# Gated cross-attention and mixture-of-experts block: nine groups in place of ten, scores of two early groups as eight feature planes summed by TensorE, late value sums in pairwise additions, and a planner that counts VectorE's dependent instructions apart

## The chip, the cores and the metric

The kernel runs on one core of a Trainium2 chip. The metric is device time in microseconds (us) of one execution; a kernel's time is the median of several executions. The engines are named TensorE (PE in the profile; PEld is its weight load), VectorE (DVE), ScalarE (ACT), GpSimd (POOL) and SyncE (SP), which here issues most transfers.

## The reference

The input is 8192 tokens of 128 features, and a context of the same shape. Each token is normalised and attends, **within itself**, over 16 heads of 8 features: query head i sees key heads 0 to i of its own token's context. The result, times tanh of a gate, is added to the token. Then comes a feed-forward part on the normalised sum: one shared expert for all tokens, and 8 experts of which each token takes its two best.

```
qh = layernorm(x).reshape(B, S, 16, 8);  kh = vh = ctx.reshape(B, S, 16, 8)
scores = einsum("bsqd,bskd->bsqk", qh, kh) / sqrt(8), causal over the 16 heads
x = x + tanh(g_xattn) * (softmax(scores) @ vh)
xf = layernorm(x);  logits = xf @ router_w.T + bias;  two best, softmax of the two
x = x + tanh(g_ffn) * (shared(xf) + sum over the two best e of w_e * expert_e(xf))
expert(z) = (silu(z @ w1) * (z @ w3)) @ w2        # 128 -> 256 -> 128
```

All is float32.

## The kernel before

**Groups.** The tokens are cut into groups; a group holds J tokens in each of the 128 partitions (J is 4 or 8, so a group is 512 or 1024 tokens). `STAGES` and `DENSE` (lines 32 and 33) list the J of each: stage 0 is 4, 4, 8, 8, 8, stage 1 is 8, 8, 8, 4, and one dense group of 4 comes last, ten groups in all, numbered 0 to 9.

**Attention** (`attention`, line 587). The causal 16 x 16 head pairs are taken as squares of side s = 8, 4, 2, 1 (half of them lies in the later heads, `late`), and the diagonal, called level 0: 136 pairs per token, in 1088 products. For each square VectorE multiplies query by key into a tile `pr` of up to 2048 columns (from a packed copy `qc` of the queries, made by ScalarE), and reduces over the 8 features into `sc` by a second VectorE instruction. For a group in `EARLY` (line 1298: group 2) the products are written feature by feature instead (`spread`), and TensorE sums them: eight matmuls with the identity into one PSUM tile, which ScalarE copies to `sc`. After the softmax's maxima and exponentials VectorE multiplies the weights by the values (`valued`, line 709, again into `pr`), and TensorE adds these up into the PSUM tile `o`, one identity matmul per key. For the pairs of group and level in `ON_DVE` (line 1307) VectorE reduces over the keys first, by a strided reduction into a tile `hb`, and TensorE adds only the totals.

**Rest of a group** (`rest`, line 866): output, second norm, transposes, router, then the shared expert in pieces of 512 tokens. The reciprocal root of a norm runs on GpSimd (`pow`), or, for the entries of `NEWTON` (line 1304), as eleven small VectorE instructions. `dispatch` gives each token copy its slot; 2J indirect transfers issued by GpSimd put the rows into the region `xs` of their expert.

**Blocks.** `plan` (line 1021) finds out, by a chain of small VectorE instructions, which blocks of 128 rows are complete. `block_pair` (line 1105) handles two blocks: SyncE fetches rows `xb` and the expert's weights `wb` (384 KB a block), TensorE transposes and multiplies, ScalarE applies silu and scales the result `yb`, and GpSimd puts the rows to `ys` by two indirect transfers. Blocks become available group by group: 8, 16, 16, 32 after groups 1 to 4, and 8, 16, 16, 24 after groups 5 to 8 (lines 418 to 426), 136 in all. When a stage's last group has been planned, `finish` (line 1222) adds `ys` into each group's tokens, two accumulating transfers per group, and stores them. The dense group runs all eight experts on all of its tokens, with `xT` at hand, and needs no dispatch.

**Order.** Every operation is recorded with an engine, a modelled duration and a priority, and `Recorder.order` (line 152) writes the order of every engine's instructions at build time: on each engine it starts the ready operation of the lowest priority value. A priority is a time in units of one group of 8 (`when`, line 1248), plus offsets by kind (`NORM`, `STATS`, `PLAN`, `BLOCKS`, `PUT`, `REST`, `SHARED`, `DLAG` and `DSTEP`) and by hand (`SHIFT`, line 1311). The engines run these orders as written; each waits in order. A buffer pool (`CT`, `PR`, `PM`, `YB` and others, line 1300) bounds how far ahead they may run.

Of the kernel before, what the change touches and what calls it, by code (L numbers as in the profile page):

```python
# [20 lines left out]
P = 128  # L21
# [10 lines left out]
STAGES = [[4, 4, 8, 8, 8], [8, 8, 8, 4]]  # L32
# [5 lines left out]
NORMED = [[0], [1], [2], [3, 4], [5, 6], [7, 8, 9]]  # L38
# [72 lines left out]
class Op:  # L111
    def __init__(self, eng, emit, us, lat, prio, table, size):
        self.eng, self.emit, self.us, self.lat = eng, emit, us, lat
        self.prio, self.table, self.size = prio, table, size
        self.deps, self.behind, self.next, self.new = set(), set(), [], []
        self.ins, self.start, self.end = [], None, None
        self.put = False


class Recorder:  # L120
# [6 lines left out]
    def add(self, eng, emit, us, r=(), w=(), after=(), behind=(), lat=0.06, table=None, size=0):  # L127
        self.prio += 1e-5
        op = Op(eng, emit, us, lat, self.prio, table, size)
# [22 lines left out]
    def order(self):  # L152
# [30 lines left out]
        while len(done) < len(self.ops):  # L183
# [43 lines left out]
            for n in op.next:  # L227
                same = n.eng == op.eng and not op.size
                ready[n] = max(ready[n], t + us if same or op in n.behind else op.end)
                todo[n] -= 1  # L230
                if not todo[n]:
                    wait[n.eng].append(n)
# [11 lines left out]
def kernel(  # L244
# [66 lines left out]
    def fixed(eng, handle, base, per):  # L311


        class Calls:
            def __getattr__(self, method):
                def call(out, *a, n=0, us=None, table=None, behind=(), **k):
                    w = [out] + ([k["accum_out"]] if "accum_out" in k else [])
                    r = list(a) + [v for name, v in k.items() if name != "accum_out"]
                    return record(
# [4 lines left out]
                        us if us is not None else base + per * n,  # L324
                        r, w, table=table, behind=behind,
# [4 lines left out]

    V = fixed(DVE, nc.vector, 0.13, 1.045e-3)
    A = fixed(ACT, nc.scalar, 0.14, 0.88e-3)
    G = fixed(POOL, nc.gpsimd, 0.2, 2.4e-3)

# [180 lines left out]
    tabled = record(DVE, tables, 2.5, [], [])  # L515
# [4 lines left out]
    def stats(parts, which):  # L520
# [10 lines left out]
        def sums(fn, dst, **k):  # L531
            i = 0
            for g, src, scratch in parts:
                for j in range(JS[g]):
# [3 lines left out]
                        to, src[:, j, :], fn, accum_out=dst[:, i : i + 1].part(g), us=0.4,  # L538
                        **bias, **k,
# [27 lines left out]
    def normed(dst, src, g, rs, mb):  # L567
        for j in range(JS[g]):
            A.activation(
                dst[:, j, :], src[:, j, :], AF.Identity,  # L570
                bias=mb[:, j : j + 1], scale=rs[:, j : j + 1], us=0.4,
# [4 lines left out]
    def first_norm(g):  # L576
        q_[g] = buf("q", [P, JM, D])[:, : JS[g]]
        normed(q_[g], xs_[g], g, *norms.pop(g))
# [8 lines left out]
    def attention(g):  # L587
        J = JS[g]
        first = len(R.ops)
        q, ct = q_.pop(g), ct_.pop(g)  # L590
        sc = buf("sc", [P, JM * NS])

        qc = {}
        for s in (8, 4, 2):
            qc[s] = buf(f"qc{s}", [P, JM * NH // 2, HD], bufs=1)[:, : J * NH // 2]
            A.copy(
                qc[s].rearrange("p (t s) d -> p t s d", s=s), halves(q, s)[0], n=J * D // 2
            )
# [11 lines left out]
        def spread(pr, pattern, **k):  # L610


            if g in EARLY:
                pr = pr.rearrange("p (d n) -> p n d", d=HD)
                return pr.rearrange("p (a k) d -> p a k d", **k) if k else pr
            return pr.rearrange(pattern, d=HD, **k)

        def summed(dst, pr, n):

            if g not in EARLY:  # L620
                pr = pr.rearrange("p (n d) -> p n d", d=HD)
                V.tensor_reduce(dst, pr, AX.X, ALU.add, n=n * HD)
                return

            acc = psum("m", [P, n], PM)
            matmuls(
                [
                    (acc, ident, pr[:, d * n : (d + 1) * n], d == 0, d == HD - 1)
                    for d in range(HD)
                ],  # L630
                1.75e-3 * n * HD,
            )
            A.copy(dst, acc, n=n)

        for s in SQ:
            T = J * NH // (2 * s)
            n = T * s * s
            parts = max(1, n * HD // PRW)
            hi, lo = halves(q, s)[0], halves(ct, s)[1]
            for h in range(parts):  # L640
                t0, tn = h * T // parts, T // parts
                a0, an = h * n // parts, n // parts
                pr = products()[:, : an * HD]
                if s > 1:
                    V.tensor_tensor(
                        spread(pr, "p (a k d) -> p a k d", k=s),
                        qc[s][:, t0 * s : (t0 + tn) * s]
                        .unsqueeze(2).to_broadcast([P, tn * s, s, HD]),
                        lo[:, t0 : t0 + tn]
                        .rearrange("p t k d -> p t (k d)")  # L650
                        .unsqueeze(2)
                        .to_broadcast([P, tn, s, s * HD]),
                        ALU.mult, n=an * HD,
                    )
                else:
                    V.tensor_tensor(
                        spread(pr, "p (t d) -> p t d"), hi[:, :, 0], lo[:, :, 0],
                        ALU.mult, n=an * HD,
                    )
                summed(level(sc, s)[:, a0 : a0 + an], pr, an)  # L660
        pr = products()[:, : J * D]
        (G if g in ON_POOL else V).tensor_tensor(
# [707 lines left out]
```

## Time and profile before

| | us |
|---|---|
| median of 9 runs (684.32 to 695.59) | 690.8 |
| the profiled execution | 687.88 |
| its span | 686.2 |
| TensorE busy | 542.2 |
| VectorE busy | 484.6 |
| GpSimd busy | 361.2 |
| ScalarE busy | 342.7 |

The mean clock granted to TensorE was 0.916 of full speed. The span begins with the first instruction and ends with the last, so 1.7 us of the execution lie around it.

The page gives busy time by engine and by fortieths of the span. Other views used below: the table of stretches (busy time of each engine in given windows, with the granted clock, the share of the transfer engines and their rate), the groups of instructions by form (mean duration of one), the order of time, and the chain that ended last. Groups are written `out<-in`. Nearly all instructions carry line 321 or 345, the helpers that record them, so tiles identify them.

### The profile page before, as it was taken

The page shows a single profiled execution, that of the slowest core. Times are in us where ns is not written, and L with a number is a line of the kernel's source. Part 1 is how long each engine was busy: PE and PEld are TensorE (multiplying, and loading weights), DVE is VectorE, ACT ScalarE, POOL GpSimd, SP SyncE. Part 2 cuts the span into 40 slices and gives each one's busy share as a digit, 9 for nine tenths or more (in the row PEclk, how much of TensorE's full clock was granted, in tenths as well). Part 3 has the DMA queues.
Part 4 walks back from the last instruction along what each step waited for, and adds up shares of the span by engine and source line. Part 5 has one row for each costly group of instructions (what it writes and reads, how often), then busy time and mean ns, then how long its engine had stood idle before and what let it go on. Part 6 is the DMA issues. An engine that isn't in the chain of part 4 may idle for free.

```text
span 686.2 us, 10993 instructions
## 1 busy us (share of the span) xinstructions
PE 542.2 (79%) x3247; PEld 450.2 (66%) x3247; DVE 484.6 (71%) x964; ACT 342.7 (50%) x1085; POOL 361.2 (53%) x342
## 2 busy tenths in 40 slices
PE   0075977968958977998797289996776879999997
PEld 0053865856846767796587278885564778988764
DVE  1698938999987995799597077999964863423343
ACT  6277467186158275856662028826433515544321
POOL 2020744526824874478758734577676374555440
PEclk9996987979989998999899589999787999999999
DMA  9710200521366227621868147489375388888095
GB/s 166 257 31 0 106 19 25 188 78 36 127 217 208 62 92 226 204 100 40 260 191 263 56 124 240 154 168 269 118 217 174 126 270 261 276 271 277 26 174 164
DMA packets 62716, 107.34 MB, mean 156 GB/s; under 512 B 10137, under 2 KB 34216, under 8 KB 62656
## 3 DMA queue, kind: packets, MB, share of 16 engines
q1 hardware_dynamic: 51424, 82.88, 38.8%
q0 software_dynamic: 10784, 23.74, 12.8%
q8 instruction: 26, 0.43, 0.3%
q14 instruction: 34, 0.28, 0.1%
q10 hardware_dynamic: 448, 0.01, 0.0%
HBM read 85.48 MB, written 25.31 MB: 161 GB/s over the span
## 4 chain that ended last, share of the span: by engine, by line
PE 41%; DVE 18%; POOL 13%; DMA 8%; issue 7%; another core or an unknown queue 5%; ACT 5%; SPq 3%; POOLq 0%; DVEq 0%; ACTq 0%
PE m L345 14%; PE gp L345 10%; PE up L345 10%; POOL xs L842 8%; DVE pr L321 5%; PE o L345 5%; DMA x<-ys 3%; DVE sc L321 2%; PE m L343 2%; DVE hb L321 2%; ACT xm L321 2%; POOL rsaw L321 1%; SPq L507 1%; POOL ys L1205 1%
## 5 line engine op out<-in xcount | busy, mean ns | idle before, releaser
L842 POOL DMA_INDIRECT xs<-xm,slot x120 | 158.9, 1324 | 65.7 <-issue 35.4
L345 PE MATMUL o<-pr,ident 128*128 128x256 f32 (+1 forms) x452 | 118.0, 414 | 33.9 <-DVE pr L321 33.5
L1205 POOL DMA_INDIRECT ys<-yb,xb x80 | 86.9, 1086 | 92.3 <-ACT yb L321 73.6
L345 PEld LDWEIGHTS o<-pr,ident 128*128 128x128 f32 x452 | 87.4, 200 | 50.8 <-DVE pr L321 32.7
L321 ACT ACTIVATE sg<-gp 128x512 f32<-128x512 f32 x116 | 68.7, 596 | 91.5 <-PE gp L345 43.4
L321 DVE TENSOR_TENSOR hb<-sg,up 128x512 f32<-128x512 f32 x68 | 46.3, 684 | 78.0 <-remote 19.9
L345 PE MATMUL m<-wb,hb 128*128 128x128 f32 x544 | 79.1, 293 | 25.5 <-DVE hb L321 7.6
L345 PEld LDWEIGHTS m<-wb,hb 128*128 128x128 f32 x544 | 71.8, 203 | 39.8 <-ACT xbT L321 9.2
L1205 POOL DMA_INDIRECT ys<-yb,seen x56 | 62.4, 1114 | 62.1 <-ACT yb L321 52.0
L345 PE MATMUL gp<-xbT,wb 128*128 128x128 f32 x544 | 78.5, 291 | 16.6 <-issue 13.1
L345 PEld LDWEIGHTS gp<-xbT,wb 128*128 128x128 f32 x544 | 72.0, 206 | 20.5 <-issue 14.3
L321 DVE TENSOR_TENSOR pr<-sc,ct 128x2048 f32<-128x2048 f32 (+3 forms) x56 | 79.1, 1441 | 4.8 <-ACT sc L321 2.9
L345 PE MATMUL up<-xbT,wb 128*128 128x128 f32 x544 | 74.9, 282 | 3.9 <-DVE hs L321 3.9
L321 ACT ACTIVATE yb<-m,xb 128x128 f32<-128x128 f32 x136 | 42.4, 363 | 60.6 <-PE m L345 38.6
L345 PEld LDWEIGHTS up<-xbT,wb 128*128 128x128 f32 x544 | 69.4, 199 | 4.6 <-DVE hs L321 4.1
L321 DVE TENSOR_REDUCE sc<-pr 128x256 f32<-128x2048 f32 (+3 forms) x50 | 71.0, 1420 | 1.0
L321 DVE TENSOR_TENSOR pr<-qc,ct 128x2048 f32<-128x2048 f32 (+2 forms) x36 | 70.1, 1953 | 0.0
L321 DVE TENSOR_TENSOR hs<-sg,up 128x512 f32<-128x512 f32 x48 | 32.3, 683 | 21.8 <-PE up L345 11.8
L321 ACT COPY qc<-q 128x512 f32<-128x512 f32 (+1 forms) x30 | 15.4, 533 | 62.5 <-DVE pr L321 62.4
L343 PE MATMUL m<-ident,xb 128*128 128x128 f32 x136 | 27.9, 284 | 21.4 <-DMA xb<-xs 13.6
L321 ACT COPY xbT<-m 128x256 f32<-128x256 f32 x68 | 24.4, 371 | 38.3 <-PE m L343 22.3
L345 PEld LDWEIGHTS m<-w2s,hs 128*128 128x128 f32 x256 | 36.2, 222 | 7.6 <-issue 5.2
(157 smaller groups left out, 897.6 us busy)
## 6 DMA issues: line engine op xcount, KB each, us to landing
wb<-wall SPq DMA_DIRECT2D x136, 384.0 KB
xb<-xs SPq DMA_DIRECT2D x136, 65.0 KB
x<-ys POOLq DMA_DIRECT2D x12, 512.0 KB
x<-in_x_dram SPq DMA_DIRECT2D x6, 512.0 KB
ct<-in_ctx_dram SPq DMA_DIRECT2D x6, 512.0 KB
out_dram<-x SPq DMA_DIRECT2D x6, 512.0 KB
pr<-wall SPq DMA_DIRECT2D x8, 384.0 KB
wall<-in_L_ffn_w_dram SPq DMA_DIRECT2D x2, 1024.0 KB
```

What stands on the lines that cost most here:

```text
L321: lambda: getattr(handle, method)(real(out), *[real(v) for v in a], **{q: real(v) for q, v in k.items()}),
L343: got.append(nc.tensor.transpose(o, a, b))
L345: got.append(nc.tensor.matmul(o, a, b, start=j[3], stop=j[4]))
L507: nc.sync.dma_start(out=wall[:, :, 2 * H + c * D : 2 * H + (c + 1) * D], in_=w2[:, c * P : (c + 1) * P, :],)
L842: ins = nc.gpsimd.indirect_dma_start(out=xs[s][:, :], out_offset=bass.IndirectOffsetOnAxis(ap=real(slot[:, i : i + 1]), axis=0), in_=real( ...
L1205: ins = nc.gpsimd.indirect_dma_start(out=ys[s][:, :], out_offset=bass.IndirectOffsetOnAxis(ap=real(ids[i]), axis=0), in_=real(yb[:, i, :]) ...
```

## The change

- `STAGES` becomes 4, 8, 8, 8 and 8, 8, 8, 8, with the dense group of 4 last: nine groups, 0 to 8. Blocks become available as 16, 16, 32 after groups 1 to 3 and 8, 16, 16, 32 after groups 4 to 7, 136 in all.
- `EARLY` is groups 1 and 2. For these, `first_norm` writes the queries with the feature outermost, ScalarE copies the keys in the same order, and `planes_scores` multiplies plane by plane; TensorE sums the eight planes of a level in one PSUM tile.
- `ON_DVE` goes. `PRE` lists, by group and level, how many rounds of pairwise additions VectorE does on `pr`, in place, each halving what TensorE adds.
- The three buffers `qc` become one; `ON_POOL`, which was empty, goes; pieces of the shared expert adapt to J.
- The planner: a VectorE or ScalarE operation's modelled time is now 0.085 or 0.09 us shorter towards an independent successor, and 0.05 us longer than its full time towards one on the same engine that depends on it (`own`). Some modelled durations change.
- `NEWTON` for the second norms grows from groups 0, 2, 6, 8 to groups 1, 2, 4, 5, 6, 7, 8. `YB` goes from 6 to 5. All offsets and `SHIFT` are replaced.

```diff
-STAGES = [[4, 4, 8, 8, 8], [8, 8, 8, 4]]
+STAGES = [[4, 8, 8, 8], [8, 8, 8, 8]]
-NORMED = [[0], [1], [2], [3, 4], [5, 6], [7, 8, 9]]
+NORMED = [[0], [1], [2, 3], [4, 5], [6, 7, 8]]
...
                 same = n.eng == op.eng and not op.size
-                ready[n] = max(ready[n], t + us if same or op in n.behind else op.end)
+                if op in n.behind:
+                    then = t + us
+                elif same:
+                    then = t + us + op.own
+                else:
+                    then = op.end
+                ready[n] = max(ready[n], then)
...
+                    early = 0.0 if "accum_out" in k else own
...
-                        us if us is not None else base + per * n,
-                        r, w, table=table, behind=behind,
+                        (us if us is not None else base + per * n) - early,
+                        r, w, table=table, behind=behind, own=early + 0.05, lat=early + 0.06,
...
-    V = fixed(DVE, nc.vector, 0.13, 1.045e-3)
-    A = fixed(ACT, nc.scalar, 0.14, 0.88e-3)
+    V = fixed(DVE, nc.vector, 0.15, 1.045e-3, 0.085)
+    A = fixed(ACT, nc.scalar, 0.14, 0.88e-3, 0.09)
...
     def first_norm(g):
...
+        q = q_[g].rearrange("p j x -> p (j x)").rearrange("p (d j s) -> p d j s", d=HD, j=J)
+        rs, mb = norms.pop(g)
+        for j in range(J):
+            A.activation(
+                q[:, :, j, :], xs_[g][:, j, :].rearrange("p (s d) -> p d s", d=HD), AF.Identity,
+                bias=mb[:, j : j + 1], scale=rs[:, j : j + 1], us=0.57,
+            )
...
+        def planes_scores():
+            qd = q.rearrange("p j x -> p (j x)")
+            cd = buf("qc", [P, 3, JM * NH // 2, HD], bufs=1).rearrange("p i t d -> p (i t d)")[:, : J * D]
+            A.copy(
+                cd.rearrange("p (d t) -> p d t", d=HD),
+                ct.rearrange("p j (t d) -> p d (j t)", d=HD), n=J * D,
+            )
+            for s in [*SQ, 0]:
+                n = J * (PAIRS[s] if s else NH)
+                acc = psum("m", [P, n], PM)
+                parts = max(1, n * HD // PRW)
+                w = HD // parts
+                for h in range(parts):
+                    pr = products()[:, : n * w]
+                    a, b = (t[:, h * w * J * NH : (h + 1) * w * J * NH] for t in (qd, cd))
+                    if s:
+                        a, b = (
+                            t.rearrange("p (x w s) -> p x w s", w=2, s=s)[:, :, i]
+                            for t, i in ((a, 1), (b, 0))
+                        )
+                        X = w * J * NH // (2 * s)
+                        if s > 1:
+                            a = a.unsqueeze(3).to_broadcast([P, X, s, s])
+                            b = b.unsqueeze(2).to_broadcast([P, X, s, s])
+                            pr4 = pr.rearrange("p (x q k) -> p x q k", q=s, k=s)
+                        else:
+                            pr4 = pr.rearrange("p (x s) -> p x s", s=1)
+                        V.tensor_tensor(pr4, a, b, ALU.mult, n=n * w)
+                    else:
+                        V.tensor_tensor(pr, a, b, ALU.mult, n=n * w)
+                    matmuls(
+                        [
+                            (
+                                acc, ident, pr[:, d * n : (d + 1) * n],
+                                h == 0 and d == 0, h == parts - 1 and d == w - 1,
+                            )
+                            for d in range(w)
+                        ],
+                        1.7e-3 * n * w + 0.01 * w,
+                    )
+                A.copy(level(sc, s)[:, :n], acc, n=n)
+
+        (planes_scores if g in EARLY else rows_scores)()
...
-                if (g, s) in ON_DVE:
-                    total = buf("hb", [P, PRW // 4], bufs=HB)[:, : an // s * HD]
-                    V.tensor_reduce(
-                        total.rearrange("p (a d) -> p a d", d=HD),
-                        pv.rearrange("p a k d -> p a d k"), AX.X, ALU.add, n=an * HD,
+                for _ in range(PRE.get((g, s), 0)):
+                    terms //= 2
+                    V.tensor_tensor(
+                        pv[:, :, :terms], pv[:, :, :terms], pv[:, :, terms : 2 * terms], ALU.add,
+                        n=an * HD * terms // s,
                     )
...
-EARLY = [2]
+EARLY = [1, 2]
-CT, PR, PM, XB, XR, YB, SG, XT, HB = 2, 5, 2, 4, 6, 6, 2, 2, 2
-PUT, REST = 1.36, 0.69
+CT, PR, PM, XB, XR, YB, SG, XT, HB = 2, 5, 2, 4, 6, 5, 2, 2, 2
+PUT, REST = 0.58, 0.61
-NEWTON = [("b", 0), ("b", 2), ("b", 6), ("b", 8)]
+NEWTON = [("b", 1), ("b", 2), ("b", 4), ("b", 5), ("b", 6), ("b", 7), ("b", 8)]
-ON_DVE = [(7, 8), (8, 2), (8, 8), (9, 4)]
+PRE = {
+    (4, 2): 1, (4, 8): 1, (5, 2): 1, (5, 8): 2, (6, 2): 1,
+    (6, 4): 2, (6, 8): 2, (7, 2): 1, (8, 4): 2, (8, 8): 3,
+}
-NORM, SHARED, BLOCKS = 0.8, 0.3, 0.25
-DSTEP, DLAG, STATS, PLAN = 0.06, 0.78, 1.4, 0.38
+NORM, SHARED, BLOCKS = 1.19, 0.16, 0.33
+DSTEP, DLAG, STATS, PLAN = 0.12, 0.3, 1.42, -0.2
...
```

The `SHIFT` table goes from 22 entries to 23 others; for the blocks of the last planned group it has no entry before (group 8) and -0.27 after (group 7).

## The prediction

> **What bounds the kernel now.** I read the busy times and the fortieths on the page first, then the table of stretches, then the order of time where a stretch looked odd, then the groups by form for durations.
>
> ```profile
> PE 542.2 (79%) x3247; PEld 450.2 (66%) x3247; DVE 484.6 (71%) x964; ACT 342.7 (50%) x1085; POOL 361.2 (53%) x342
> PE   0075977968958977998797289996776879999997
> DVE  1698938999987995799597077999964863423343
> PEclk9996987979989998999899589999787999999999
> ```
>
> No engine is full, and the two rows show why: VectorE is near 9 up to the middle, TensorE from three quarters on. The table of stretches, cut at 525 us, gives the sizes (columns: window, its length, busy us and instructions of each engine, granted clock, transfer share, GB/s):
>
> ```profile
> 0.00:525.00 525.00, 392.58 (x2248) 327.59 (x2249) 410.52 (x776) 278.52 (x927) 290.48 (x271) 0.90 0.47 140
> 525.00:686.20 161.20, 149.64 (x1000) 122.56 (x999) 74.11 (x189) 64.15 (x158) 70.69 (x72) 0.97 0.70 209
> 0.00:126.00 126.00, 71.24 (x303) 56.46 (x304) 86.89 (x188) 74.03 (x306) 43.41 (x59) 0.89 0.30 83
> ```
>
> So there are two regimes. From 525 us on TensorE is idle for only 11.6 us: the end is what TensorE still has to do. Before that it is idle for 132.4 us, and VectorE, busy 78% of the time, sets the pace with its chains. The third row is the start: the first expert block is fetched at 126.4 us, and until then TensorE lacks 55 us of work. A microsecond is gained by getting VectorE through its groups sooner, so that blocks come sooner, or by taking TensorE work out of the end.
>
> One piece belongs to neither. In the order of time VectorE waits twice near 380 us, and the chain that ended last calls both waits unknown:
>
> ```profile
> 373.10 9.16 another core or an unknown queue
> 383.10 13.24 another core or an unknown queue
> ```
>
> Both waits are on TensorE's results, which the profile takes for done at 373.7 us. A shorter one lies at 516.95 us (6.78 us), and one at 422 us (3.8 us). I can't name their cause; the change doesn't address them.
>
> **The change part by part.** Durations are of the profiled execution.
>
> ```profile
> L321 DVE TENSOR_TENSOR pr<-qc,ct 128x2048 f32<-128x2048 f32 x22 | 54.5, 2485 | 0.0
> L321 DVE TENSOR_REDUCE sc<-pr 128x256 f32<-128x2048 f32 x19 | 43.4, 2282 | 0.3
> L321 DVE TENSOR_REDUCE hb<-pr 128x256 f32<-128x2048 f32 x3 | 11.5, 3848 | 0.0
> L321 DVE TENSOR_TENSOR x<-x,xT 128x1024 f32<-128x1024 f32 x6 | 7.3, 1225 | 0.2
> L321 DVE SCALAR_TENSOR_TENSOR rsb<-tb,rsb 128x8 f32<-128x8 f32 x6 | 1.0, 167 | 0.2
> ```
>
> *Scores of groups 1 and 2.* A group of 8 reduces three times 2048 columns (2.28), twice 1024 (1.22) and once 512 (0.68): 9.97 us, which group 1 now gives to TensorE. Group 2 had given it away already, but paid for its layout: its wide products took 3.7 us (order of time, 71.43 to 83.0), against 2.29 for the others, so three times 1.4, plus 0.7 each for two of 1024 columns: 5.7 us. Planes are written in order, so I price them as the ordinary products and take 5.7 off: VectorE -15.7. Bound on the other side: the new inputs are repeated along an axis, which no row shows; if every plane product ran at the rate of the strided reduction (3.85 for 2048), 2 x 4.25 x 1.56 = 13.3 come back, leaving -2.4. I take -15.7, as the old `qc` products also repeat an input and take 2.29. TensorE gets eight planes of 1088 columns: in the end stretch 512 columns step at 0.43 us in two passes each, so 14.6 us; group 2 needed 20.2 us for the same at a lower clock. This lies where TensorE lacks work (the 55 us), so I cost it at nothing; if that cover is gone it is 15 to 20.
>
> *ScalarE* now reads the 16 columns of queries, and writes the key copies, with a stride; no row has that on ScalarE. Below: the 0.49 us of a normal column. Above: the strided VectorE reduction's factor, 1.69, on 16 x 0.49 + 2 x 1.05: 7 us. The three `qc` copies that go (0.62 each) pay for half. ScalarE is busy 53% before 525 us; I take 0, and keep +7. [...]
>
> *Value sums.* One value matmul of 256 columns steps at 0.43 us in its two passes (567.13 to 570.59 for sixteen halves). `ON_DVE` spares TensorE 14+1+7+3 = 25 of them and costs VectorE 14.2 us (11.5+2.0+0.7, the strided rows). `PRE` spares 56 and costs 21 additions; at the row of `x<-x,xT` (1.22 for 1024, 0.69 for 512 columns; a product of 256 takes 0.42) that is 18.1 us. Net: VectorE +3.9, TensorE -13.4, of which 7 matmuls, -3.0, lie in the last groups and so in the full stretch.
>
> *One group fewer.* Groups of 4 took 34 us from output to output (48.9 to 82.8, 466.8 to 500.6), groups of 8 51 to 57; two of 4 cost 68 where one of 8 costs 52. Of the 16 us about 11 are VectorE's fixed part: some 70 instructions (33 attention, 23 routing, 20 planning, less what grows) at 0.16 us, the part that doesn't shrink when 64 columns become 32 (0.22 to 0.19). The other 5 are waits.
>
> *Norms.* Three more chains of eleven at 0.167: VectorE +5.4. The waits of VectorE for GpSimd's second norms (7.7 us in four) mostly go: -2 after what else is late.
>
> *Chains counted apart.* Small dependent instructions start 0.03 us after the one before has ended; the independent `seen` at 382.95 starts 0.09 us before the `hb` of 382.35 ends. So each dependent pair that the planner fills spares 0.12 us; about 40 a group in nine groups make 43 us at most, 0 at least. I take a fifth of the pairs, since the planner must have something ready: -8.6, and at VectorE's part in the pace about -5.
>
> [...]
>
> *Later first blocks, fewer buffers.* Group 1 has 8 columns, so its rows go out later: 18 us more attention (52 against 34), less the 10 of its reductions, plus eight puts at 1.27 us, some 18, bounds 0 and 24. TensorE has the 14.6 us of planes and the larger group's value sums and shared expert (some 12) meanwhile. I take +10, nearer the lower end for that cover. `YB` of 5 lets ten blocks of results, not twelve, wait behind a burst of GpSimd's puts (16 x 1.27 = 20 us); I count that inside the same bound.
>
> **The sum.** VectorE: -15.7 + 3.9 - 11 + 5.4 = -17.4, counted at its 78% share before 525 us: -13.6. Merging's waits -5, chains -5, TensorE's end -3, norm waits -2, late blocks +10: -18.6. From 687.9 for the profiled execution that is 669.3; the median of the runs lies 2.9 higher, so I predict **672 us**.
>
> **The rivals.**
>
> *The end grows (slower).* After the last dispatch 32 blocks are left instead of 24. A pair takes 2.9 us of TensorE in the end stretch (gp, up and m 0.89 each, transposes 0.22), so 8 blocks are 11.6 us. And the stage can only be added up after its last result: before, that took from the last put at 649.70 to the output at about 677, 28 us, hidden under dense experts until 682.9. Dense experts now rank from 8.30 on, the last blocks at 8.50 (before 8.78 and 8.63), so two of eight experts run ahead of them and six, 6 x 5.22 = 31 us, are left as cover. It decides once the last put leaves less than 28 us of dense work behind it: then up to 25 us show, with the 11.6 a time of 700 to 725; I put it at 708. For it: cover shrinks to 3 us. Against it: dense weights come from `wall` at the same rate as before.
>
> *It changes nothing.* TensorE's work is 542 us before and about 543 after (+14.6, -13.4). If the planes end up on the critical path, as they partly did in group 2 (the chain has 8.7 us of its score matmuls at 97 us, at a granted clock of 0.78 in 100 to 125), VectorE's gain turns into a wait for TensorE, and the time stays at 690.
>
> *Much faster.* The unnamed waits of 30 us don't recur and the order fills the chains: 640 to 648.
>
> **How the numbers follow.** The measurement tells about 1% from no change, 684 to 698. Forecast (648 to 684): 0.55; much faster: 0.06; nothing: 0.14; end grows or another loss of its size: 0.25. For 8 in 10 the range takes the forecast, the unchanged case and the lower half of the slow one, up to 708, and stops at 646 below: with all of VectorE's 17.4 (-4), a third of the pairs (-5), no late blocks (-10) and a quarter of the unnamed waits gone (-7). Faster 0.61, same 0.14, slower 0.25.
>
> **What would show it.** Right: `pr` plane products of 2048 columns near 2.3 us; no `hb<-pr` rows, `pr<-pr` additions near 1.2; VectorE near 465 us busy; first block near 145 us; outputs of groups of 8 about 48 us apart; TensorE's full stretch begins near 505 us. Wrong: the last ys put less than 28 us before the end; a stretch before 150 us with TensorE under half busy for longer than now; unknown waits of over 30 us.

## The result, and the profile after

The kernel after takes **706.3 us** (median, 703.22 to 713.59) where the kernel before took 692.0 beside it: the ratio is **1.0241**, with a 95% interval of 1.0217 to 1.0266. The change makes the kernel slower by 2.4%; 672 us was forecast. Ratios, here and below, are of the executions in the faster of the two states that executions show, and need not equal the quotient of two medians. The profiled execution of after has a span of 705.6 us, 19.4 more than before.

Busy time and fortieths of the page of after:

```profile
PE 530.4 (75%) x3233; PEld 432.9 (61%) x3233; DVE 444.3 (63%) x940; ACT 347.1 (49%) x1079; POOL 343.1 (49%) x328
...
PE   0099996856998796398828999951698098999993
...
DVE  1693968999589797099826999960654034232342
```

The table of stretches of after, cut where that of before was cut (window, length, busy us and instructions of PE, PEld, DVE, ACT, POOL, granted clock, transfer share, GB/s):

```profile
0.00:126.00 126.00, 81.88 (x385) 62.05 (x386) 83.02 (x153) 83.21 (x314) 30.64 (x50) 0.97 0.31 87
0.00:525.00 525.00, 384.56 (x2247) 313.35 (x2247) 383.58 (x764) 286.95 (x927) 267.98 (x250) 0.91 0.45 138
525.00:705.60 180.60, 145.88 (x986) 119.51 (x986) 60.76 (x176) 60.16 (x152) 75.13 (x78) 0.92 0.64 192
```

VectorE is busy for 40.3 us less than before, TensorE for 11.8 less and GpSimd for 18.1 less; only ScalarE has 4.4 more. There is less work, and the kernel takes longer. The fortieths (17.6 us each) say where: VectorE's row has 0, 2, 0 and 0 in the slices from 282, 353, 476 and 547 us, and TensorE's row falls to 3, 2, 1 and 0 there. Before has one such place, near 377 us. In order of time, the chain that ended last names them ("another core" can't be meant, since the kernel runs on one: it is a releaser that the profile doesn't show):

```profile
276.35 8.54 another core or an unknown queue
...
286.84 10.68 another core or an unknown queue
...
477.20 20.57 another core or an unknown queue
...
547.74 14.82 another core or an unknown queue x2
...
592.33 6.11 another core or an unknown queue
```

These are 60.7 us, against 33.0 in the chain of before. The end of the longest, in the order of time of all engines:

```profile
490.92 0.96 POOL L891 DMA_INDIRECT xs<-xm,slot  x1 [0.30 <-issue]
...
492.18 0.96 POOL L891 DMA_INDIRECT xs<-xm,slot  x1 [0.30 <-issue]
493.44 0.96 POOL L891 DMA_INDIRECT xs<-xm,slot  x1 [0.30 <-issue]
...
497.79 0.75 DVE L331 SCALAR_TENSOR_TENSOR x<-m,tgf,x 128x512 f32<-128x512 f32 x1 [20.59 <-remote]
497.88 0.60 ACT L331 ACTIVATE sg<-gp 128x512 f32<-128x512 f32 x1 [19.79 <-remote]
```

VectorE and ScalarE both wait for matmuls that the profile takes for done at 476.9 and 477.8 us. GpSimd alone goes on, one put every 1.27 us, 22 of them from 466.5 us on; 3.4 us after the last has ended, both engines start within 0.1 us of each other. The other long pauses lie in such rows too: 22 puts from 266.4, 18 from 350.7, 18 from 537.0 us (steps of up to 1.6 us counted in). Before's worst pause lay in a row of 20, from 368.1 us.

So I split the span of every profile into three: the **common pauses** (stretches of over 0.3 us, after 130 us and before TensorE's last matmul, in which TensorE, VectorE and ScalarE all stand; ScalarE's loads of its function tables, 24 of 1.28 us each in after, don't count as work), the **end** (from TensorE's last matmul to the end of the span), and the **rest**. Beside them stand the **late puts**, those that follow at least eight others in a row with less than 1.45 us from start to start.

| | span | common pauses | end | rest | late puts |
|---|---|---|---|---|---|
| before | 686.2 | 22.7 | 4.4 | 659.1 | 14 |
| after | 705.6 | 62.4 | 11.6 | 631.6 | 38 |
| difference | +19.4 | +39.7 | +7.2 | -27.5 | +24 |

The experiments ask whether the rows of puts cause the pauses, which edit made the rows, and what the change is worth without them.

### The profile page after: what moved, and what is told of

Read it like the earlier page. It is cut to its first block, busy times and chain, and to the rows that moved or that the text cites. A ratio compares the mean times of both kernels' runs of the same rounds, so it can differ in the third digit from the quotient of the medians.

```text
span 705.6 us, 10927 instructions
## 1 busy us (share of the span) xinstructions
PE 530.4 (75%) x3233; PEld 432.9 (61%) x3233; DVE 444.3 (63%) x940; ACT 347.1 (49%) x1079; POOL 343.1 (49%) x328
## 4 chain that ended last, share of the span: by engine, by line
PE 50%; DVE 15%; another core or an unknown queue 9%; issue 8%; ACT 8%; DMA 4%; SPq 3%; POOL 2%; ACTq 0%; DVEq 0%
PE m L355 18%; PE gp L355 11%; PE up L355 10%; PE o L355 9%; DVE pr L331 5%; DVE sc L331 3%; PE m L353 2%; POOL xs L891 2%; ACT q L331 2%; ACT junk L331 1%; ACT xm L331 1%; SPq L517 1%; DVE hb L331 1%; DMA x<-in_x_dram 1%
## 5 line engine op out<-in xcount | busy, mean ns | idle before, releaser
L891 POOL DMA_INDIRECT xs<-xm,slot x120 | 151.4, 1261 | 87.0 <-issue 38.7
L355 PE MATMUL o<-pr,ident 128*128 128x256 f32 (+1 forms) x400 | 114.2, 435 | 45.9 <-DVE pr L331 45.1
L1256 POOL DMA_INDIRECT ys<-yb,xb x72 | 80.2, 1114 | 96.7 <-ACT yb L331 78.4
L355 PEld LDWEIGHTS m<-wb,hb 128*128 128x128 f32 x544 | 70.3, 199 | 89.0 <-DVE hb L331 52.8
L355 PEld LDWEIGHTS o<-pr,ident 128*128 128x128 f32 x400 | 79.3, 208 | 63.5 <-DVE pr L331 40.3
L1256 POOL DMA_INDIRECT ys<-yb,seen x64 | 74.8, 1169 | 75.5 <-ACT yb L331 63.5
L355 PE MATMUL gp<-xbT,wb 128*128 128x128 f32 x544 | 74.2, 281 | 0.3 <-ACT xbT L331 0.3
L355 PEld LDWEIGHTS gp<-xbT,wb 128*128 128x128 f32 x544 | 69.2, 197 | 6.1 <-issue 4.6
L331 DVE TENSOR_REDUCE sc<-pr 128x256 f32<-128x2048 f32 (+3 forms) x40 | 60.1, 1504 | 0.0
L331 DVE TENSOR_TENSOR pr<-qc,ct 128x2048 f32<-128x2048 f32 (+2 forms) x26 | 48.3, 1874 | 11.2 <-PE o L355 5.8
L331 ACT COPY xbT<-m 128x256 f32<-128x256 f32 x68 | 25.4, 373 | 60.8 <-PE m L353 32.9
L355 PE MATMUL m<-w2s,hs 128*128 128x128 f32 x256 | 37.8, 308 | 15.0 <-ACT yb L331 9.9
L353 PE MATMUL m<-ident,xb 128*128 128x128 f32 x136 | 30.2, 282 | 16.4 <-DMA xb<-xs 16.4
```

The lines of the kernel that those rows point to most:

```text
L331: lambda: getattr(handle, method)(real(out), *[real(v) for v in a], **{q: real(v) for q, v in k.items()}),
L353: got.append(nc.tensor.transpose(o, a, b))
L355: got.append(nc.tensor.matmul(o, a, b, start=j[3], stop=j[4]))
L891: ins = nc.gpsimd.indirect_dma_start(out=xs[s][:, :], out_offset=bass.IndirectOffsetOnAxis(ap=real(slot[:, i : i + 1]), axis=0), in_=real( ...
L1256: ins = nc.gpsimd.indirect_dma_start(out=ys[s][:, :], out_offset=bass.IndirectOffsetOnAxis(ap=real(ids[i]), axis=0), in_=real(yb[:, i, :]) ...
```

## The experiments

### The puts by themselves

In outline, only this is left of the kernel, in eight phases with different puts:

```
for i in range(puts):                       # GpSimd
    nc.gpsimd.indirect_dma_start(out=dst[:, :], out_offset=...slot[:, i:i+1]..., in_=row)
    if every and i % every == every - 1:
        nc.gpsimd.tensor_tensor(junk8, junk8, half8, ALU.pow)
for i in range(chain):                      # TensorE and ScalarE, one after the other
    nc.tensor.matmul(m, ident, a, start=True, stop=True); nc.scalar.copy(a, m)
```

> The suspected cost by itself: of the computation nothing is left but copying x to the output. Beside it a chain of 100 links, a TensorE matmul of 128 columns and a ScalarE copy that waits for it (some 0.8 us a link), and GpSimd's puts of 128 rows in eight phases: 30 links without puts; 24 puts in a row; 24 puts with a pow of 8 columns (1.7 us) after every fourth; 24 puts of which every fourth waits until the one before it has landed; 24 puts in a row beside 16 loads of 384 KB; 24 in a row beside VectorE products of 1024 columns, one every third link; both; and the loads with a pow after every fourth put. Theory A (a row of puts without a break holds TensorE's signals back until 3 us after its last put): in the phases with 24 unbroken puts the chain stands still for 10 to 20 us at least once, and in those with pows or landings it does not, or for under 3 us. Rival B (the transfers of rows and weights are what holds it): a standstill only in the phases with loads. Rival C (the puts run unbroken because VectorE stands, not the other way round): no standstill over 2 us in any phase.

| phase (24 puts) | us from put to put | longest link |
|---|---|---|
| in a row | 1.27 | 3.50, from the 19th put on |
| pow after every 4th | 1.62 | 1.15 |
| in a row, with loads | 1.26 | 4.91, from the 13th put on |
| in a row, beside VectorE products | 2.00 | 1.15 |
| in a row, loads and VectorE products | 1.60 | 4.91 |
| loads, pow after every 4th | 1.62 | 1.15 |

Theory A holds in kind, and B and C fall: puts in a row are enough, without loads, to stretch a link from 1.15 to 3.5 us, and a pow among them is enough to stop that, with loads too. Its size was wrong: the chain never stood for the 10 to 20 us that were written, and no link lost more than 3.8 us. (The waits for landings of a fourth phase, with links of up to 4.19 us, don't appear in GpSimd's instructions, so it was one more unbroken row.) VectorE's products stretch a put from 0.96 to 1.97 us, and then no link is long. With the loads, VectorE waits for their buffers between 650 and 660 us, no product runs, and the long links are back. Here the slower puts are the harmless ones.

### Breaks in the kernel

The edit goes into the loop that emits the order; the orders of the other engines stay as they are:

```diff
+                if op.put and len(run) >= 4:
+                    for _ in range(1):
+                        space = nc.gpsimd.tensor_tensor(spare, spare, mhalf[:, :8], ALU.pow).ins
+                        for b in run:
+                            tc.add_manual_dep(space, b.name, ORDER, reason="order")
+                        prev, run = space, [space]
+                    run = []
```

> The kernel after, with one more GpSimd instruction after every fourth put in a row: a pow of 8 columns on a spare tile, 1.7 us. It only adds work, 20 to 40 us of GpSimd. Theory A: the four pauses of TensorE, VectorE and ScalarE (276 to 297, 358 to 372, 478 to 498, 547 to 562 us, about 70 us in the chain) shrink to under 15 us together, and the kernel falls to 660 to 685 us. Rival B (transfers or instruction fetches hold TensorE's signals): the pauses stay, 705 to 715. Rival C (the pause has its cause elsewhere and the puts only fill it): the same, 705 to 715.

> The kernel before, with the same pow after every fourth put in a row. It has three rows of 8 puts or more: 20 from 368 us, 8 from 498, 10 from 510, and pauses of 34 us in all. Theory A: these pauses go, 20 to 30 us are won less some 5 for puts that come later, 660 to 680. Rivals B and C: 690 to 700, pauses as before.

After with breaks took 695.9 us, 1.0074 of before (1.0041 to 1.0107); before with breaks 714.0, 1.0322 (1.0271 to 1.0374). The mechanism was right and its price was not. VectorE's waits of unknown origin fell from 57.7 to 4.3 us in after and from 33.2 to 5.1 in before. But 62 pows take 1.9 us each in after (59 in before), and now the tokens' rows come late: TensorE waits 58.1 us for transfers of `xb`, 16.4 without the pows (in before 37.0 against 13.6). The three engines still stand together for 41.5 us in e2, without one late put: common pauses have other causes too. VectorE's waits put down to no named engine, in e2, and the pows among the groups of e2:

```profile
DVE x L331 <- remote: 4.3, 1, 4.3
```

```profile
L1346 POOL TENSOR_TENSOR spare<-spare,mhalf 128x8 f32<-128x8 f32 x62 | 117.5, 1896 | 0.7
```

> The kernel after, with every fifth put in a row waiting until the put before it has landed (some 2 us), and no more work. Theory A in the form that puts still in flight hold the signals: the pauses shrink as with a pow, 660 to 690 us. If it is the writing of the puts itself on GpSimd and a wait of 2 us is too short a break, the pauses stay and the time is 700 to 720. Rivals B and C: pauses as they were, 705 to 720.

The edit is a dependence of every fifth put on the one before. It took 708.7 us, 1.0252 (1.0181 to 1.0323), but tells nothing of puts in flight: GpSimd has no more waiting instructions than in after (182 against 183). It is one more run of after. Whether it is the writing of the puts or the puts in flight that does the harm, no run tells.

### Another chip

The next four kernels ran on a chip on which **before takes 645.7 us**, not 690.

> What break is enough. Of the computation nothing is left but copying x to the output; beside it the chain of TensorE matmul and ScalarE copy (1.15 us a link), 60 links a phase, and six phases of 24 puts and 16 loads of 384 KB: unbroken; a pow of 8 columns (1.8 us) after every 8th put; after every 12th; an iota of 8 columns (0.2 us) after every 4th; after every 2nd; after every put. Unbroken I expect links of 4 to 5 us from about the 12th put on. If what counts is the room that a break gives (something fills up a little faster than it empties), the pow after 8 keeps all links under 2 us, the pow after 12 leaves one or two long links, the iota after every put (cadence 1.6 us) has none and the iota after every 4th (cadence 1.35) has some. If what counts is only that a row is interrupted, the iota after every 4th has none either.

All six phases had links of 1.15 us, the unbroken one with loads as well. What was written assumed long links there, and fell with them.

> The kernel after, with the pow of 8 columns after every eighth put in a row instead of every fourth: at most half of the added GpSimd work (63 pows took 113 us there). If puts held up by the pows are what is left of the loss (695.9 us with a break after four) and eight puts in a row are still harmless, 675 to 692 us, unknown waits under 20 us in the chain. If rows of eight already hold the signals beside this traffic, 695 to 706.

> The kernel after with one constant put back: PUT 1.36 instead of 0.58, so that GpSimd's puts of a group rank 0.78 of a group earlier. If the rank of the puts made the long rows (they then run beside VectorE's small instructions, at 0.96 us a put, instead of beside its wide products, which stretch a put to 2 to 4 us), the puts beyond the 8th of an unbroken row fall from 38 to under 20 as in the kernel before (14), and the time to 670 to 695. If the rows come from other parts (the norms taken from GpSimd, the groups of 8), they stay at over 30 and the time at 700 to 712.

> The kernel after with NEWTON as before (second norms of groups 0, 2, 6 and 8 on VectorE, the others by pow on GpSimd). If the pows that left GpSimd were what broke the rows, the puts beyond the 8th of a row fall from 38 to under 20 and the time to 675 to 698, though VectorE waits for GpSimd's norms again. If not, they stay over 30 and the time is 703 to 715.

The three took 661.7, 646.6 and 644.1 us: 1.0248 (1.0219 to 1.0276), 1.0021 (0.9996 to 1.0046) and 0.9979 (0.9961 to 0.9997) of before. None has a wait of unknown origin on VectorE or ScalarE. Breaks only cost here: in e6 30 pows hold GpSimd for 55.8 us, and TensorE waits 45.6 us for `xb`. In e7 the puts go on unbroken, 47 in a row from 459.7 us, and TensorE does not notice (table of stretches):

```profile
459.00:520.00 61.00, 58.91 (x386) 46.47 (x385) 34.81 (x123) 28.95 (x78) 46.16 (x48) 1.00 0.71 229
```

So what these three were meant to tell stayed open. But a new theory, A2, came of them: the rows hold up TensorE on some chips only. To see whether the two go together, the second measurement of the puts by themselves was run again, with both kernels:

> The puts and the chain alone, the same kernel as the second such measurement (links of 1.15 us throughout, even beside 24 unbroken puts and 16 loads of 384 KB), to see which kind of chip these runs are on. Before's median was 690 us where the chain was held up beside unbroken puts (links of up to 4.91 us) and 646 us where it was not. Theory A2 (puts in a row hold TensorE's signals back on some chips and not on others): before at 685 to 700 us here goes with links of over 2 us beside unbroken puts, before at 640 to 655 us with links of 1.15 us only, and nothing else. Rival: the two do not go together, and the 45 us between the chips have another cause. Where links are long, the phases with breaks tell which break is enough: the pow after 8 puts and the iota after every put I expect to keep them under 2 us.

> The kernel after as it is, beside before. Theory A2: where TensorE's signals are held up (before at 690), it is 2.4% slower again, 703 to 710. Where they are not (before at 646), its rows of 18 to 22 puts cost nothing, the unknown waits leave the chain (61 us of it in the profile of after, 33 in that of before), and the change shows what its instructions are worth: 630 to 645 us, a ratio of 0.975 to 1.00. Rival (the change itself is slow, by its order, with or without the held signals): 655 to 665 where before is at 646.

> The kernel before once more, for its profile. Where signals are held up: pauses as in its first profile, unknown waits of about 33 us in the chain. Where they are not: a span of 640 to 650 us, no unknown wait of over 2 us in the chain, and long rows of puts without any pause.

Here before took 690.6 us, and the links were long again. In order of time, in the unbroken phase of e9:

```profile
24.27 0.27 ACT L127 COPY a<-m 128x128 f32<-128x128 f32 x1 [3.61 <-remote]
24.52 0.96 POOL L101 DMA_INDIRECT xs<-row,slot  x1 [0.30 <-issue]
...
24.59 0.80 PE L125 MATMUL m<-a,ident 128*128 128x128 f32 x2 [3.08 <-issue]
...
29.18 0.27 ACT L127 COPY a<-m 128x128 f32<-128x128 f32 x1 [4.64 <-remote]
```

and 70 us later, with a pow after every eighth put:

```profile
95.49 0.27 ACT L127 COPY a<-m 128x128 f32<-128x128 f32 x1 [0.89 <-issue]
...
95.81 0.80 PE L125 MATMUL m<-a,ident 128*128 128x128 f32 x2 [0.35 <-issue]
...
96.64 0.27 ACT L127 COPY a<-m 128x128 f32<-128x128 f32 x1 [0.89 <-issue]
```

One direction of the link is delayed. ScalarE's copy ends at 24.54 us and TensorE starts at 24.59, as always. TensorE's matmul ends by the profile at 25.39, and ScalarE starts 3.8 us later (0.03 us in the phase with pows). Whether the matmul itself or its signal is late, no run tells; "held signals" stands for either below.

Of the breaks, the pow after every 8th put and after every 12th kept all links at 1.15 us. An iota of 0.2 us did not: 4.20 us after every 4th put, 3.51 after every 2nd, 2.81 after every one. Interrupting a row isn't enough. The break may have to give time, or to be another kind of instruction: the mean step hardly differs (1.34 us with a pow after every 12th put, 1.32 with an iota after each), and a long break of another kind was not tried. After took 709.2 us, 1.0284 (1.0194 to 1.0373), with common pauses of 62.7 us and an end of 11.5; before's profile has 23.3 and 4.4.

### Fewer breaks, and PUT alone

Here the break comes after eight puts that the order plans with less than 2 us between them:

```diff
+                if op.put:
+                    row = row + 1 if op.start - last < 2.0 else 1
+                    last = op.start
+                    if row == 8:
+                        ...                      # the same pow; row = 0
```

> The kernel after, with a pow of 8 columns (1.8 us) after every eighth put, counted only within rows that the order itself plans without a gap of 2 us: 17 pows, against 63 with a pow after every fourth. Theory: where signals are held (before at 690), no unknown wait over 5 us is left in the chain, GpSimd is 30 us busier, and the time falls from 706 to 655 to 680, below before. Where they are not held (before at 646) it costs 0 to 10 us, 635 to 660. Rival (eight in a row beside this traffic hold the signals already): 690 to 706 with pauses of 10 us left.

> The kernel before with the same break in its rows. Where signals are held: its three pauses go and it falls from 690 to 665 to 685. The forecast of the change without the pauses was -2.7%: after with breaks over before with breaks should be 0.96 to 0.99 on either chip. Rival (the change's engine work isn't what sets its time): 1.00 or more.

> The kernel after with PUT back at 1.36, as in e7, for a chip that holds signals. If the later rank of the puts made the harmful rows: unknown waits under 30 us in the chain and 665 to 692 us where before is at 690. If not: 700 to 712. Where before is at 646: 643 to 650 again.

> The kernel before with PUT at 0.58 instead of 1.36, and nothing else. If the later rank of the puts makes the harmful rows, the puts beyond the 8th of an unbroken row rise from 14 to 25 or more, and where signals are held the time to 700 to 720, with 15 to 30 us more of unknown waits. If not, the rows stay and the time is 688 to 700. Where before is at 646: 645 to 660, since blocks come later.

These four ran together, on a chip with before at 687.8 us:

| | ratio (interval) | us | common pauses | end | rest | late puts |
|---|---|---|---|---|---|---|
| e12: after, 19 pows | 1.0013 (0.9973 to 1.0053) | 686.1 | 32.2 | 12.8 | 633.0 | 4 |
| e13: before, 17 pows | 0.9955 (0.9907 to 1.0003) | 685.3 | 14.9 | 4.4 | 663.9 | 0 |
| e14: after, PUT 1.36 | 1.0502 (1.0441 to 1.0563) | 721.1 | 60.9 | 27.1 | 633.8 | 33 |
| e15: before, PUT 0.58 | 1.0018 (0.9973 to 1.0063) | 687.6 | 12.5 | 9.2 | 666.3 | 6 |

The last four columns are of the profiled execution, which can lie some us from the median (e12's took 679.7).

Nothing but pows is added in e12, and the loss is gone: by the ratios, rows of puts cost after 2.3%, some 16 us of its 706. That is causal, since no other engine's order changed. It is less than expected: a row of 12 is left (454.8 to 469.0 us; the real spacing is not the planned one), and 32 us of common pauses. VectorE's waits of unknown origin are 32.8 us, 57.7 in after, and the expectation that none over 5 us stays in the chain failed. One of those left lies beside a row of exactly eight puts, from 534.8 us on:

```profile
538.32 1.06 PE L355 MATMUL up<-xbT,wb 128*128 128x128 f32 x8
...
543.71 0.99 POOL L1256 DMA_INDIRECT ys<-yb,xb  x1 [0.30 <-issue]
...
544.83 0.69 DVE L331 TENSOR_TENSOR hb<-sg,up 128x512 f32<-128x512 f32 x1 [7.28 <-remote]
```

VectorE starts 5.4 us after the matmul that it reads has ended by the profile, and 0.1 us after the last put. So the rival written for e12, that eight in a row hold signals beside this traffic, is true in part. With breaks in both kernels, after over before is 1.001 by the medians (1.006 by the ratios), not 0.96 to 0.99.

The rank of the puts is not the cause. Put back in after, it leaves the pauses and lengthens the end; moved in before, it makes the rows shorter, not longer. Both expectations on it were wrong. Late puts are no measure of the harm either: e15 has 6 of them, but 40.9 us of waits of unknown origin in its chain, before 33.0.

e14 is the same kernel as e7. It tied with before where signals aren't held (1.0021) and is 5% slower here, and nothing but the chip differs. That fits held signals as the cause of the 5%, though the two chips may differ in more than that.

### The norms

> The kernel after as it is, a third time, in the hope of a chip that doesn't hold signals. There (before at 646): 628 to 642 us, faster by 1 to 3%, as its time outside the common pauses of TensorE, VectorE and ScalarE says (645.1 us against 663.5 in the two first profiles); rival: 646 to 660, the rest of the change is worth nothing. Where signals are held (before at 690): 703 to 710.

> The kernel after with NEWTON as before, as in e8. Where signals are held: if the pows that left GpSimd made the harmful rows, the time in which the three engines stand together after 130 us falls from 60 to under 35 us and the time from 706 to 675 to 692; if not, it stays over 50 and the time at 700 to 715. Where they are not held: 642 to 647 again.

> The same with a pow of 8 columns after every eighth put that the order plans without a gap. Where signals are held: common pauses under 30 us and 670 to 688, which would beat both kernels (690 and 706). Where they are not: 645 to 660, since the pows only cost.

e17 undoes one constant; e18 adds the breaks of e12:

```diff
-NEWTON = [("b", 1), ("b", 2), ("b", 4), ("b", 5), ("b", 6), ("b", 7), ("b", 8)]
+NEWTON = [("b", 0), ("b", 2), ("b", 6), ("b", 8)]
```

| | ratio (interval) | us | common pauses | end | rest | late puts |
|---|---|---|---|---|---|---|
| e16: after | 1.0279 (1.0204 to 1.0353) | 710.6 | 66.2 | 11.6 | 630.3 | 44 |
| e17: after, NEWTON as before | 0.9970 (0.9924 to 1.0017) | 687.4 | 36.7 | 17.0 | 624.4 | 26 |
| e18: the same, 18 pows | 0.9931 (0.9893 to 0.9970) | 684.7 | 32.9 | 17.1 | 633.0 | 5 |

Before was at 689.7 us here, so e16 could not tell what after does on the other kind of chip. NEWTON alone takes 23 us off after and 29.5 off its common pauses, which leaves 36.7 where under 35 was written (34.7 if table loads count as work, as they did in the 60 of the expectation), and a time inside the range that was. So without this one edit the change is no loss; whether another single edit would do the same was not tried. Two explanations remain for how: its pows no longer break the rows of puts, or the planner's whole order shifts with it. The second isn't excluded, since all orders differ, and rows of 18 puts are left in e17. e18 is faster than both kernels, by 0.7% over before; its breaks take 21 late puts away but only 3.8 us of common pauses. The kernel of e17 stands level with before on both kinds of chip (e8: 0.9979).

## Why the prediction was wrong

**The step that failed is the one that cost nothing.** The prediction found before's unnamed waits, 33 us in the chain, wrote that "the change doesn't address them" and left them as they were. With breaks in the rows of GpSimd's puts nearly all of VectorE's unnamed waits go (57.7 to 4.3 us in e2), in before too (33.2 to 5.1 in e4), so they come from those rows. The change moved seven second norms off GpSimd instead of four and wrote a new order, in which the puts of four groups follow each other unbroken. The common pauses grew by 39.7 us, twice the whole loss; breaking the rows alone, in e12, took off some 16 us, the whole loss. I priced the three more `NEWTON` chains at VectorE +5.4 and -2 of waits, and never asked what GpSimd does in the freed time: another put, 0.3 us after the last. Before's own trace had the clue, 20 puts at 368.1 to 392.4 us around the two longest unknown waits:

```profile
368.11 0.96 POOL L842 DMA_INDIRECT xs<-xm,slot  x1 [0.30 <-issue]
...
382.35 0.69 DVE L321 TENSOR_TENSOR hb<-sg,up 128x512 f32<-128x512 f32 x1 [9.25 <-remote]
...
392.43 0.97 POOL L1205 DMA_INDIRECT ys<-yb,seen  x1 [0.30 <-issue]
...
396.36 0.96 DVE L321 RECIPROCAL rd<-m 128x128 f32<-128x128 f32 x1 [13.26 <-remote]
```

The "51 to 57" us from output to output of a group of 8 left this stretch out: in before two such groups are 73.7 and 93.4 us apart, from 242.3 to 409.4 us, and one later 70.3.

**The engines' work went as forecast, or better.** The groups by form, in after:

```profile
L331 DVE TENSOR_TENSOR pr<-q,qc 128x2048 f32<-128x2048 f32 x6 | 13.4, 2286 | 0.0
...
L331 DVE TENSOR_TENSOR pr<-pr 128x1024 f32<-128x1024 f32 x8 | 9.5, 1207 | 0.0
...
L331 ACT ACTIVATE q<-x,mba,rsa 128x128 f32<-128x128 f32 x12 | 6.4, 565 | 2.8 <-DVE mba L331 2.8
...
L331 ACT COPY qc<-ct 128x1024 f32<-128x1024 f32 x2 | 4.1, 2046 | 1.1 <-DVE pr L331 1.0
...
L331 ACT COPY xm<-xm 128x1024 f32<-128x1024 f32 x7 | 7.3, 1045 | 0.1
...
L355 PE MATMUL m<-pr,ident 128*128 128x512 f32 x32 | 14.1, 592 | 0.0
```

- *Planes.* A product of 2048 columns takes 2.286 us, as priced, though its inputs repeat; the dear bound of 3.85 is out. TensorE's plane sums (four forms, 14.1, 7.9, 7.2 and 4.0) are 33.2 us for two groups, 13.0 more than before; 14.6 was forecast. Up to 178 us TensorE stands for 63.0 us, before 64.5: they lie where it lacked work.
- *ScalarE.* The strided key copy takes 2.05 us, nearly twice the 1.05 of a plain one; of the twelve `q<-x,mba` eight are strided, 0.60 each if the four plain ones take 0.49. ScalarE's total is 4.4 us higher, between the bounds of 0 and 7.
- *Value sums.* The 21 pairwise additions take 17.7 us (18.1 forecast), and no `hb<-pr` is left.
- *VectorE in all.* Its instructions add up to 526.9 us before and 507.4 after: -19.5, forecast -17.4.
- *Chains counted apart.* Busy time fell by 40.3, so 20.8 us more are overlapped (63.1 against 42.3). I took 8.6, a fifth of the pairs at 0.12 us; 20.8 us are about half. The bound of 43 was right, the value too small.
- *Late blocks.* The first block is fetched at 176.1 us, not 145. I charged +10; with TensorE standing no longer than before up to then, it seems to cost about nothing; no run undoes it alone.

Without that +10 my sum was -28.6 us; the rest in the table, with pauses and end taken off, is -27.5. That is an agreement of sums and no proof: an engine that has stood catches up later, and pauses and rest are not independent.

**The rival "the end grows" came true in part.** Its cause is as described: the dense work no longer covers the way from the last put to the output. The last put starts 21.6 us before TensorE's last matmul ends, before 32.0. That is less than 28, so the condition that the prediction set for this rival was met. The way from the last put to the issue of the last merged output was priced well (28 us; it is 26.6, before 25.5). Left out were the 6.6 us from there to the end of the span, which lay under TensorE's dense work before:

```profile
672.42 0.97 POOL L1256 DMA_INDIRECT ys<-yb,seen  x1 [0.30 <-issue]
...
688.60 0.87 POOL L1281 DMA_DIRECT2D x<-ys  x1 [1.64 <-DMA x<-ys]
...
695.22 0.35 SPq L1066 DMA_DIRECT2D out_dram<-x  x1
...
695.66 3.73 SPq L1294 DMA_DIRECT2D out_dram<-x  x4
```

The last of the four merged outputs (`x4`) goes out at 699.05 us, when its merging transfer has landed; in before at 675.2, with 6.6 us of dense work still to come. So the end is 11.6 us instead of 4.4, and in relatives of after that have fewer pauses it is longer: 16.9 in e8. There, in order of time, TensorE is done while the merging transfers still run, and four outputs wait on SyncE for 9.39 us:

```profile
622.48 1.83 PE L355 MATMUL m<-pr,hs 128*128 128x128 f32 x14 [0.63 <-DVE hs L331]
...
624.83 0.86 POOL L1281 DMA_DIRECT2D x<-ys  x1 [2.09 <-DMA x<-ys]
...
625.50 0.35 SPq L1066 DMA_DIRECT2D out_dram<-x  x1
...
627.02 9.39 SPq L1294 DMA_DIRECT2D out_dram<-x  x4
```

The term "TensorE's end -3" looked at matmuls and missed this. It is also where part of the gain goes once the pauses are gone: in e8 the common pauses are 18.2 us and the end 16.9, in a span of 641.2, level with before on that chip.

**Of the signs named beforehand**, the planes, the additions and the missing `hb<-pr` were right. VectorE's 465 us came out as 444. The outputs of groups were to be 48 us apart and are 40 to 84 (34 to 93 in before). TensorE is full from 600 us on (93.4 us busy of the 94.0 to its last matmul's end), not 505. Of the signs of a wrong forecast, the unknown waits of over 30 us came; the last put was 33 us before the end and not under 28, but the end grew all the same, since it is the 21.6 us of dense work behind the put that count.

**What stays open.** After itself was never run on the chip where before takes 646 us; two relatives, e7 and e8, tied with before there, whose own profile was not taken on it. So a gain of the whole change without pauses isn't shown, only that its engine work is smaller. Nor is it shown that held signals explain all of the 45 us between the chips.

## What to carry to other kernels

An unknown wait in the kernel before is part of the sum: look at what every engine does during it, the ones off the path too, and ask whether the change makes more of it. Taking work off GpSimd is not free when what remains is a row of its own transfers: where before took 690 us, links beside puts at 1.27 us without a break grew from 1.15 to 3.50 us from the 19th put on, with loads to 4.91 us from the 13th on (e1), and in this kernel VectorE started 5.4 us late beside a row of eight (e12). A pow after every eighth put of such a row won back the loss here (1.0013 of before in e12, 1.0241 without it); one after every fourth ended nearly all of the waits and cost more than it won in before (1.0322 in e4). It belongs only where the row is really unbroken.

## What was not expected of the hardware

- Beside an unbroken row of GpSimd's indirect puts ScalarE starts up to 3.8 us after the matmul that it waits for has ended by the profile (a link takes 4.91 instead of 1.15 us, e9), and VectorE stands for 20.6 us so in the kernel (after, from 477.2 us). TensorE isn't late: it starts 0.05 us after ScalarE's copy has ended (e9).
- By themselves, long links set in after 18 puts without other transfers and after 12 with loads of 384 KB (e1). With slower puts (1.97 us beside VectorE's products, e1) or a pow of 1.7 us after 4 puts (e1), and in e9 with a pow after 8 or 12, every link took 1.15 us; with an iota of 0.2 us after each put they reached 2.81 us (e9). In the kernel a late start is seen beside a row of eight (5.4 us in e12).
- It differs from chip to chip. On the chip with before at 645.7 us the same phases show links of 1.15 us throughout (e5) and the kernel 47 unbroken puts with TensorE busy for 58.9 of 61 us (e7); on the others, where before took 688 to 692 us, every profile of after has common pauses (62.4, 62.7 and 66.2 us) and so have those of before (22.7 and 23.3), and the puts alone had links of up to 4.91 us in both measurements (e1, e9).
